# The first layer of a two-layer adaptive FFN: one written order for every engine, clamps moved to GpSimd, zero products in gaps, and pads spread over blocks

## The chip, the cores and the metric

The kernel runs on one core of one Trainium2 chip. The metric is the device time of one execution in microseconds, the median of several runs. TensorE is called PE here (its weight loads PEld), VectorE DVE, ScalarE ACT, GpSimd POOL; SyncE, which issues most transfers, is SP.

## The reference, cut to what matters

The input x has 8 batches of 512 tokens with 256 features. Two layers follow each other, each with a residual.

```python
# layer 0: a LoRA of the batch's language, then a fake-quantized FFN
y    = (x @ A[lang].T) @ Bm[lang].T + emb[lang]
xq   = round(y / sx) clipped to -128..127, times sx       # sx from max |y| over ALL of y
gate = xq @ wq(w_gate).T ; up = xq @ wq(w_up).T           # 704 columns, weights quantized by row
h    = silu(gate) * up
hq   = the same rounding, with a scale from max |h| over ALL of h
x    = x + hq @ wq(w_down).T
# layer 1: an adapter with a layer norm, then 9 experts of which each token takes 2
z = layernorm(x + relu(x @ W1 + b1) @ W2 + b2) * gamma + beta
x = x + sum over the top 2 of 9 experts of weight * (silu(z @ Wg) * (z @ Wu)) @ Wd
```

The two maxima over everything split layer 0 into parts that can't overlap: no element of y can be rounded before the last of y is known, none of h before the last of h.

## The kernel before, in words

Layer 0 keeps everything on the chip, with features on the 128 partitions. Batches go in four pairs (k = 0 to 3). In the LoRA part `lora_in(k)` makes the rank products of a pair into one two-bank PSUM tile, ACT masks them to the pair's languages (`t`), `lora_out` multiplies back, and ACT adds the embedding into `y_pairs`. DVE takes the maximum of each pair into `ymax`. Meanwhile the weights come in twice: raw by rows, from which DVE takes the row scales (`row_scales`), and transposed, which `weight_in` multiplies by the inverse scales (carried across partitions by PE in `spread`) into 16-bit integers, so that rounding happens in the conversion; a copy makes them bf16 (`wgT`, `wuT`, `wdT`). `abs_max_all` ends the part with the maximum over all partitions, and `act_scale` makes the scale `x_scale` and its inverse `x_inv`.

Rounding y is two steps: ACT writes `y * inv` as int16 into one of two buffers `v`, DVE clamps it into the bf16 tile `yq`. Gate and up are then made in chunks of 128 of the 704 columns, for one pair: five full chunks of 1024 elements a partition and a last one of 64 columns, whose two batches lie above each other (512 elements). For each chunk `gate_chunk` has eight products, `finish` takes silu on ACT, and then either DVE multiplies straight out of PSUM, or (`by_pool`, three chunks of a pair, 12 in all) ACT copies the up half out and POOL multiplies. DVE takes the maximum of each chunk into `hmax`. The four PSUM tiles rotate, as do three `g` and two `u`. The order is that in which the Python loops call these functions, and each engine works through its own share of it in order, with the scheduler switched off.

Behind the last maximum, the scale of h is made in the same way. From there a written list, `ORDER`, gives the order of all pieces: rounding of h (`qa` on ACT, `qd` on DVE), the down products (`dp`), the adapter, the routing, and the first 14 blocks of the expert stage. The routing writes each token's row, by indirect DMAs from POOL, into a list in DRAM for each of its two experts. The expert stage works on blocks of 128 rows of these lists. SP fetches for each block, in its own order: the rows (four quarters and a small `tag`), the gate and up weights (1408 KB) and the down weights (768 KB). A weight fetch is conditional: it is skipped when the buffer holds that expert already. There are three weight buffers, and rows are asked for four blocks ahead. From block 14 on, a loop calls `first_half(i)` and `second_half(i)`, in which `ask` issues the fetches.

The number of rows of an expert is known only when routing is done, so the last block of an expert has to be filled up: `write_pads` writes, for each of the nine experts, 128 rows of padding (130 KB) behind its list's end. SP reads the place from `endi` and issues the DMA. Before, all nine go out in one go ahead of block 20 (`pads_at = done + 6`):

```python
        for i in range(done, SURE):
            if i == pads_at:
                write_pads()
                asked["planned"] = NBLK
            first_half(i)
            second_half(i)
```

The list is one DRAM tensor, so that a fetch of rows waits for pads written before it, and a pad waits for rows that were fetched before it.

Of the kernel before, what the change touches and what calls it, by code (L numbers as in the profile page):

```python
# [23 lines left out]
F32 = mybir.dt.float32  # L24
# [8 lines left out]
P = 128  # L33
# [5 lines left out]

ORDER = """  # L40
# [29 lines left out]
def adaln_ffn_kernel(  # L70
# [124 lines left out]
    def rounded(dst, src, inv):  # L195

        v = in_turn("v", v_pair)
        shape = list(src.shape)[1:]
        n = shape[0] if len(shape) == 1 else shape[0] * shape[1]
        v = v[:, :n] if len(shape) == 1 else v[:, :n].rearrange("p (a b) -> p a b", b=shape[1])  # L200
        nc.scalar.activation(v, src, AF.Copy, scale=inv)
        return lambda: nc.vector.tensor_scalar(dst, v, QMAX, -QMAX - 1.0, ALU.min, ALU.max)  # L202

# [18 lines left out]

    with tc.tile_pool(name="hw", bufs=1) as hw, tc.tile_pool(
        name="wide", bufs=4, space=bass.MemoryType.PSUM
    ) as wide, tc.manual_schedule():

        def banks(name):
            return wide.tile([P, 2 * S], F32, tag="pw", name=name)


# [9 lines left out]

        taken = 0

        def piece(w, a, b):
            nonlocal taken
            raw = upper_[:, taken : taken + a * b]
            taken += a * b
            nc.sync.dma_start(raw, w)
            return raw.rearrange("p (a b) -> p a b", b=b)

        for b in range(4):  # L250
            nc.sync.dma_start(x_sb[:, b], xT[b])
        raw_g = piece(w_gate, NM, D)
        for b in range(4, B):
            nc.sync.dma_start(x_sb[:, b], xT[b])
        raw_u = piece(w_up, NM, D)
        raw_gT = piece(w_gate_T, KC, I)
        raw_uT = piece(w_up_T, KC, I)
        raw_d = piece(w_down, KC, I)
        raw_dT = piece(w_down_T, NM, D)
        assert taken <= HB // 2 * PAIR - NY  # L260
        nc.sync.dma_start(wr, Wr.rearrange("(c p) e -> p c e", p=P))
        nc.sync.dma_start(lists[E * CAP :], pad)
# [5 lines left out]

# [14 lines left out]
        hot = hw.tile([NL0, B], F32, name="hot")  # L283
        nc.vector.tensor_scalar(hot, idf[:NL0, HB:], pcol[:NL0], None, ALU.is_equal)
        emb = hw.tile([P, KC, B], F32, name="emb")
        pe = banks("pe")
        for c in range(KC):
            nc.tensor.matmul(
                pe[:, c * B : (c + 1) * B], lhsT=emb_sb[:, c * P : (c + 1) * P], rhs=hot, start=True, stop=True
            )  # L290
        nc.vector.tensor_copy(emb.rearrange("p c b -> p (c b)"), pe[:, : KC * B])
        ymax = hw.tile([P, HB], F32, name="ymax")
# [4 lines left out]
        def lora_in(k):  # L297
            pr = banks("pr")
            for c in range(KC):
                for z in range(2):  # L300
                    nc.tensor.matmul(
                        pr[z * HR : (z + 1) * HR, :S],
                        lhsT=aT[:, c],
                        rhs=x_sb[:, 2 * k + z, c],
                        start=c == 0,
                        stop=c == KC - 1,
                    )
            t = hw.tile([P, S], F32, tag="t", bufs=2, name="t")
            nc.scalar.activation(t, pr[:, :S], AF.Copy, scale=mask[:, k : k + 1])
            return t  # L310

        def lora_out(k, t):
            for c in range(KC):
                py = banks("py")
                for z in range(2):
                    zs = slice(z * HR, (z + 1) * HR)
                    nc.tensor.matmul(
                        py[:, z * S : (z + 1) * S], lhsT=bT[zs, c * P : (c + 1) * P], rhs=t[zs], start=True, stop=True
                    )
                for z in range(2):  # L320
                    b = 2 * k + z
                    nc.scalar.activation(
                        y_pairs[k][:, z, c], py[:, z * S : (z + 1) * S], AF.Identity, bias=emb[:, c, b : b + 1]
                    )


        def row_scales(name, raw, scale):

            top = hw.tile(list(scale.shape), F32, name=f"top_{name}")
            abs_max(top, raw)  # L330
            nc.vector.tensor_scalar(scale, top, 1.0 / QMAX, None, ALU.mult)
            inv = hw.tile(list(scale.shape), F32, name=f"inv_{name}")
            nc.vector.reciprocal(inv, scale)
            return inv

        def across(pi, at, col, n):

            nc.tensor.transpose(pi[:, at : at + n], col.to_broadcast([n, P]), ident[:n, :n])

        def spread(inv):  # L340
            pi = banks("pi")
            for m in range(NM):
                across(pi, m * P, inv[: rows[m], m : m + 1], rows[m])
            return pi

        def weight_in(name, raw_T, pi):
            wq = hw.tile([P, KC, I], I16, tag="wq", bufs=2, name=f"wq_{name}")
            nc.vector.tensor_tensor(wq, raw_T, pi[:, :I].unsqueeze(1).to_broadcast([P, KC, I]), ALU.mult)
            return wq.rearrange("p c i -> p (c i)")

        def abs_max_all(dst, stats, name):

            own = hw.tile([P, 1], F32, name=name)
            nc.vector.tensor_reduce(own, stats, AX.X, ALU.max)
            pi = banks("pi")
            across(pi, 0, own, P)
            nc.vector.tensor_reduce(dst, pi[:, :P], AX.X, ALU.max)

        ts = {0: lora_in(0)}
        for k in range(HB):  # L360
            if k + 1 < HB:
                ts[k + 1] = lora_in(k + 1)
            if k == 0:
                inv_g = row_scales("g", raw_g, swg)
            elif k == 3:
                inv_u = row_scales("u", raw_u, swu)
                pi_g = spread(inv_g)
                wq_g = weight_in("g", raw_gT, pi_g)
            lora_out(k, ts.pop(k))
            abs_max(ymax[:, k : k + 1], y_pairs[k].rearrange("p z c t -> p (z c t)"))  # L370
        nc.scalar.copy(wgT.rearrange("p c i -> p (c i)"), wq_g)


        ytop = hw.tile([P, 1], F32, name="ytop")
        abs_max_all(ytop, ymax, "ytop_own")
        pi_u = spread(inv_u)
        sx, rx = act_scale(ytop, sig[:, 0:1], "x")

        def round_y(b):
            return rounded(  # L380
                yq[:, b].rearrange("p c t -> p (c t)"), y_pairs[b // 2][:, b % 2].rearrange("p c t -> p (c t)"), rx
            )

        for w_scale in (swg, swu):
            nc.vector.tensor_scalar(w_scale, w_scale, sx, None, ALU.mult)
        first = round_y(0)
        second = round_y(1)
        wq_u = weight_in("u", raw_uT, pi_u)
        first()
        nc.vector.tensor_copy(wuT.rearrange("p c i -> p (c i)"), wq_u)  # L390
        second()
# [3 lines left out]
        def gate_chunk(k, m, by_pool):  # L395
            ms = slice(m * P, (m + 1) * P)
            h = h_full(k)[:, m].rearrange("p z t -> p (z t)")
            pg, pu = banks("pg"), banks("pu")
            for p, w in ((pg, wgT), (pu, wuT)):
                for c in range(KC):  # L400
                    for z in range(2):
                        nc.tensor.matmul(  # L402
                            p[:, z * S : (z + 1) * S],
                            lhsT=w[:, c, ms],
                            rhs=yq[:, 2 * k + z, c],
                            start=c == 0,
                            stop=c == KC - 1,
                        )
            finish(h, pg, pu, m, by_pool)

        def finish(h, pg, pu, m, by_pool):
            n = h.shape[1]
            g = hw.tile([P, 2 * S], F32, bufs=3, tag="g", name="g")[:, :n]
            nc.scalar.activation(g, pg[:, :n], AF.Silu, scale=swg[:, m : m + 1])  # L414
            if by_pool:
                u = hw.tile([P, 2 * S], F32, bufs=2, tag="u", name="u")
                nc.scalar.activation(u, pu[:, :n], AF.Copy, scale=swu[:, m : m + 1])  # L417
                nc.gpsimd.tensor_tensor(h, u, g, ALU.mult)  # L418
            else:
                nc.vector.scalar_tensor_tensor(h, pu[:, :n], swu[:, m : m + 1], g, ALU.mult, ALU.mult)  # L420

        def last_chunk(k):
            pg, pu = banks("pg"), banks("pu")
            for p, w in ((pg, wgT), (pu, wuT)):
# [15 lines left out]
        for k in range(HB):  # L440
# [7 lines left out]
            for second in seconds:  # L448
                second()
# [730 lines left out]
```

## Time and profile before

| what | value |
|---|---|
| median of 3 runs | 739.7 us (738.42 to 741.25) |
| profiled execution | 740.5 us, of which the profile's span is 738.4 us |
| granted PE clock, mean | 0.951 |
| PE busy | 680.9 us, 92% |
| DVE busy | 365.2 us, 49% |
| ACT busy | 203.6 us, 28% |
| POOL busy | 200.1 us, 27% |
| LoRA until `x_inv` | 0 to 33.4 us |
| gate and up until `htop_own` | 33.5 to 93.1 us |
| first down product | 98.4 us |
| one block of the expert loop on PE | 7.5 us |

The profile's lines give a start, a duration, the engine, the line of the kernel, the operation and its tiles; what stands in brackets is the idle time of the engine before it and what ended it. An SP line shows the issue of a DMA, not its transfer. PEclk is the share of full clock that PE was granted in a stretch.

### The profile page before, as it was taken

To read this page: it belongs to the slowest core of one execution; us is meant where nothing else is said; L and a number is where in the kernel's file an instruction comes from. 1 tells how busy PE (TensorE), PEld (TensorE's weight loads), DVE (VectorE), ACT (ScalarE), POOL (GpSimd) and SP (SyncE) were. 2 spreads that over 40 slices of the span, in tenths; PEclk is the share of its full clock that TensorE was granted. 3 is DMA by queue.
4 is the path that set the end of the run, shared out by engine and by line. 5 is a ranking of instruction groups with operands and counts; after the bars stand their busy time and mean duration, and the time that the engine had idled before them with its cause. 6 is when DMAs were issued, how large, how long until landed. Compare 5 with 4: busy or idle time off the path is not lost. (4 is left out here: it accounts for less than half of the span.)

```text
span 738.4 us, 14537 instructions
## 1 busy us (share of the span) xinstructions
PE 680.9 (92%) x4592; PEld 578.2 (78%) x4592; DVE 365.2 (49%) x1207; ACT 203.6 (28%) x403; POOL 200.1 (27%) x173
## 2 busy tenths in 40 slices
PE   7498669979899899899998999999999999999995
PEld 2233225536698899799997999999999999999994
DVE  3759948988957384433332333333333333333331
ACT  4577675534413031111110111111111111111110
POOL 1045500446253213452121212121212112121212
PEclk9789977879999999999999999999999999999998
DMA  9500002448757786433367623279934489135742
GB/s 347 194 1 2 0 16 64 130 166 293 257 130 235 238 261 188 76 80 42 47 166 199 162 34 44 31 209 315 296 53 106 92 275 278 30 45 151 218 98 32
DMA packets 85424, 103.44 MB, mean 140 GB/s; under 512 B 58200, under 2 KB 74720, under 8 KB 82016
## 3 DMA queue, kind: packets, MB, share of 16 engines
q1 hardware_dynamic: 72480, 85.15, 37.6%
q0 software_dynamic: 12720, 17.31, 12.2%
q8 instruction: 38, 0.62, 0.3%
q14 instruction: 42, 0.34, 0.2%
q10 hardware_dynamic: 144, 0.01, 0.0%
HBM read 176.86 MB, written 22.83 MB: 270 GB/s over the span
## 5 line engine op out<-in xcount | busy, mean ns | idle before, releaser
L974 PE MATMUL bank<-upper__104,lower 128*128 128x128 f32 x2948 | 347.3, 277 | 5.4 <-DMA lower<-in_L_ffn_W_dram 3.0
L974 PEld LDWEIGHTS bank<-upper__104,lower 128*128 128x128 f32 x2948 | 344.3, 194 | 10.0 <-issue 3.3
L1033 POOL DMA_INDIRECT out_dram<-upper__104,tag x67 | 104.5, 1560 | 373.3 <-DVE upper__104 L964 281.7
L990 DVE TENSOR_TENSOR upper__104<-bank,upper__104 128x512 f32<-128x512 f32 x67 | 46.3, 691 | 157.3 <-PE bank L974 157.3
L1023 PE MATMUL bank<-upper__104 128*128 128x256 f32 x528 | 121.4, 379 | 0.0
L1023 PEld LDWEIGHTS bank<-upper__104 128*128 128x128 f32 x528 | 97.1, 191 | 11.4
L984 ACT ACTIVATE upper__104<-bank 128x512 f32<-128x512 f32 x67 | 40.0, 597 | 233.8 <-PE bank L974 232.6
L758 POOL DMA_INDIRECT lists<-row,sloti x64 | 62.6, 979 | 97.6 <-ACT zT L672 42.1
L1000 ACT ACTIVATE upper__104<-bank 128x128 f32<-128x128 f32 x67 | 18.5, 277 | 186.1 <-PE bank L974 186.1
L1023 PE MATMUL bank<-lower,upper__104 128*128 128x256 f32 x276 | 64.0, 382 | 0.4 <-issue 0.4
L1029 DVE TENSOR_SCALAR upper__104<-bank,wt 128x256 f32<-128x256 f32 x67 | 32.4, 483 | 60.6 <-PE bank L1023 60.5
L1023 PEld LDWEIGHTS bank<-lower,upper__104 128*128 128x128 f32 x276 | 51.2, 192 | 6.9 <-issue 0.8
L1006 DVE TENSOR_TENSOR upper__104<-bank,upper__104 128x128 f32<-128x128 f32 x67 | 19.4, 290 | 71.5 <-ACT upper__104 L1001 70.3
L559 PE MATMUL bank<-yq,wdT 128*128 128x512 bf16 x80 | 25.4, 457 | 5.6 <-DVE yq L547 5.6
L414 ACT ACTIVATE g<-pg,swg 128x1024 f32<-128x1024 f32 (+1 forms) x24 | 24.8, 1048 | 9.2 <-PE pg L402 5.5
L418 POOL TENSOR_TENSOR lower<-u,g 128x1024 f32<-128x1024 f32 x6 | 14.1, 2358 | 45.8 <-ACT u L417 45.8
L402 PE MATMUL pg<-yq,wgT 128*128 128x512 bf16 x80 | 22.0, 396 | 3.7 <-DVE yq L202 2.2
L402 PE MATMUL pu<-yq,wuT 128*128 128x512 bf16 x80 | 22.1, 401 | 2.6 <-DVE lower L420 2.6
L649 ACT ACTIVATE row<-row,shift,rstd 128x256 f32<-128x256 f32 x32 | 16.8, 590 | 22.4 <-DVE shift L643 22.4
L681 PEld LDWEIGHTS bank<-wr,zT 128*128 128x128 f32 x128 | 18.3, 226 | 4.7 <-issue 3.9
L681 PE MATMUL bank<-wr,zT 128*128 128x9 f32 x128 | 18.4, 281 | 3.6 <-DVE row L623 3.4
L559 PEld LDWEIGHTS <-wdT 128*128 128x128 bf16 x80 | 8.3, 115 | 17.1 <-issue 8.0
(200 smaller groups left out, 600.9 us busy)
## 6 DMA issues: line engine op xcount, KB each, us to landing
lower<-in_L_ffn_W_dram SPq DMA_DIRECT2D x70, 1408.0 KB
upper__104<-in_L_ffn_W_dram SPq DMA_DIRECT2D x46, 768.0 KB
lower<-in_L_ffn_W_dram SPq DMA_DIRECT2D x23, 768.0 KB
lower<-lists SPq DMA_DIRECT2D x144, 32.0 KB
upper__104<-lists SPq DMA_DIRECT2D x140, 32.0 KB
x_sb<-in_x_dram SPq DMA_DIRECT2D x8, 512.0 KB
out_dram<-xtok SPq DMA_DIRECT2D x8, 512.0 KB
lists<-pad SPq DMA_DIRECT2D x10, 130.0 KB
```

The source lines that it names most:

```text
L402: nc.tensor.matmul(p[:, z * S : (z + 1) * S], lhsT=w[:, c, ms], rhs=yq[:, 2 * k + z, c], start=c == 0, stop=c == KC - 1,)
L414: nc.scalar.activation(g, pg[:, :n], AF.Silu, scale=swg[:, m : m + 1])
L559: nc.tensor.matmul(pd, lhsT=wdT[:, m, cs], rhs=hq_sb[b % 2][:, m], start=m == 0, stop=False)
L681: nc.tensor.matmul(pl[:, j * E : (j + 1) * E], lhsT=zT_sb[b % 2][:, c, j * P : (j + 1) * P], rhs=wr[:, c], start=c == 0, stop=c == KC - 1,)
L758: nc.gpsimd.indirect_dma_start(out=own_rows[(b * NJ + j) * 2 + n], out_offset=bass.IndirectOffsetOnAxis(ap=sloti_sb[b % 3][:, j, n : n + 1 ...
L974: nc.tensor.matmul(pg[:, at * P : (at + 1) * P], lhsT=gu_sb[i % NW][:, c, n * P : (n + 1) * P], rhs=xbT_sb[i % 3][:, c], start=c == 0, sto ...
L984: nc.scalar.activation(g_sb[i % 3][:, :4].rearrange("p m t -> p (m t)"), held.pop(("pg", i, "a")), AF.Silu)
L990: nc.vector.tensor_tensor(hid_sb[i % 3][:, :4].rearrange("p m t -> p (m t)"), held.pop(("pg", i, "b")), g_sb[i % 3][:, :4].rearrange("p m ...
L1006: nc.vector.tensor_tensor(hid[:, 4], pg[:, P : 2 * P], gs[:, 4], ALU.mult)
L1023: nc.tensor.matmul(po[:, :D], lhsT=hid_sb[i % 3][:, m], rhs=dn_sb[i % NW][:, m], start=m == 0, stop=m == NM - 1)
L1029: nc.vector.tensor_scalar(y_sb[i % 3], held.pop(("po", i))[:, :D], small_["wt"][i % NX], None, ALU.mult)
L1033: nc.gpsimd.indirect_dma_start(out=out, out_offset=bass.IndirectOffsetOnAxis(ap=tag_sb[i % NX][:, 0:1].bitcast(I32), axis=0), in_=y_sb[i % 3],
```

## The change

Five things change, all but the last in layer 0.

1. The LoRA, the weights and gate and up are written as small pieces with names (`li`, `t`, `lo`, `ye`, `ym` for the LoRA; `tp`, `s`, `wq`, `c` for the weights; `ox`, `tx`, `yt`, `sw` for the scale; `v`, `yr` for rounding; `gp`, `up`, `sl`, `uc`, `pm`, `st`, `mx` for the chunks; `L` for loads), and a literal list, `FRONT`, gives their order for all engines. Gate and up products of a chunk are pieces of their own, and chunks of different pairs mix. POOL multiplies 8 chunks (`pm`) instead of 12, DVE 16 (`st`). The maximum of y is taken by pair and half of the features. Row scales and weights of all three matrices now come ahead of the first product.
2. Loads are pieces too: the last pair of x is loaded behind `u`, `uT` and `gT`, and `g`, `d`, `dT` behind it.
3. Five of the eight clamps of y (`yr` with 1 at the end) run on POOL.
4. `z_n` stands for n products of a tile of zeros, written into the PSUM tile that is next in turn: 10 at the start, 6 and 2 in the LoRA, 10, 4 and 12 around the scale of y, and 12 behind the transpose that carries the maximum of h across.
5. `write_pads` becomes `write_pad(e)`, called ahead of each of the blocks 16 to 24, one pad each.

The core of the diff:

```diff
+FRONT = """
+    z_10 pe L_x0 em L_x1 z_6 li_0 L_u t_0 li_1 L_x2 lo_0_0 tp_u t_1 lo_0_1 ye_0_0 L_uT lo_1_1 ye_0_1 ym_0_0 lo_1_0
+    L_gT ye_1_1 li_2 ym_0_1 ye_1_0 ym_1_1 L_x3 s_u t_2 ym_1_0 lo_2_1 wq_u L_g lo_2_0 ye_2_1 li_3 ye_2_0 c_u L_d
+    ym_2_1 t_3 tp_g L_dT z_2 lo_3_0 lo_3_1 ye_3_0 ym_2_0 s_g ye_3_1 ym_3_0 ym_3_1 ox tp_d z_10 tx yt z_4 s_d sw v_1
+    wq_g v_0 yr_1_0 c_g yr_0_0 wq_d z_12 up_0_2 v_2 gp_0_2 v_3 c_d yr_2_1 gp_0_0 sl_0_2 gp_0_1 sl_0_0 yr_3_1 st_0_2
+    v_4 mx_0_2 up_0_0 sl_0_1 yr_4_1 up_1_0 st_0_0 v_5 up_0_1 mx_0_0 uc_1_0 gp_0_5 up_1_3 st_0_1 sl_0_5 gp_0_3
...
+    uc_3_4 up_3_3 mx_3_0 sl_3_5 gp_3_4 mx_3_2 gp_3_3 sl_3_4 mx_3_1 up_3_5 sl_3_3 pm_3_4 st_3_5 st_3_3 mx_3_3 mx_3_4
+    mx_3_5
+"""
+LAST_LOAD = "L_dT"
+ZEROS_BEHIND = 12
...
+        busy = hw.tile([P, S], BF16, name="busy")
+        nc.vector.memset(busy, 0.0)
...
+        def z(n):
+            pz = wide_sb[(turn_of.get("wide", -1) + 1) % len(wide_sb)]
+            for _ in range(n):
+                nc.tensor.matmul(pz[:, :S], lhsT=busy[:, :P], rhs=busy, start=True, stop=True)
...
+        def yr(b, by_pool):
+            (nc.gpsimd if by_pool else nc.vector).tensor_scalar(
+                yq[:, b], at.pop(("v", b)), QMAX, -QMAX - 1.0, ALU.min, ALU.max
             )
...
+        own = hw.tile([P, 1], F32, name="htop_own")
+        nc.vector.tensor_reduce(own, hmax.rearrange("p b k -> p (b k)"), AX.X, ALU.max)
+        ph = banks()
+        across(ph, own, P, 0)
+        z(ZEROS_BEHIND)
         htop = l0.tile([P, 1], F32, name="htop")
-        abs_max_all(htop, hmax.rearrange("p b k -> p (b k)"), "htop_own")
+        nc.vector.tensor_reduce(htop, ph[:, :P], AX.X, ALU.max)
...
-    def write_pads():
-        for e in range(E):
-            r = nc.sync.value_load(endi[0:1, e : e + 1], min_val=e * CAP, max_val=e * CAP + T)
-            nc.sync.dma_start(lists[ds(r, P)], pad)
+    def write_pad(e):
+        r = nc.sync.value_load(endi[0:1, e : e + 1], min_val=e * CAP, max_val=e * CAP + T)
+        nc.sync.dma_start(lists[ds(r, P)], pad)
...
-        pads_at = done + 6
+        pads_at = done + 2
         for i in range(done, SURE):
-            if i == pads_at:
-                write_pads()
+            if pads_at <= i < pads_at + E:
+                write_pad(i - pads_at)
+            if i == pads_at + E:
                 asked["planned"] = NBLK
             first_half(i)
             second_half(i)
```

## The prediction, made before the result was known

> **What bounds the kernel now.** I read the page's slices first, then the stretches that I cut at the stage borders, then the timelines of DVE, PE and SP at those borders. The chain that ended last covers only the final 18 us, so it says nothing about the stages edited here.
>
> ```profile
> PE   7498669979899899899998999999999999999995
> DVE  3759948988957384433332333333333333333331
> PEclk9789977879999999999999999999999999999998
> ```
>
> Each digit is 18.5 us. From about 300 us PE is full, and only what delays PE costs time there. In the first five slices it isn't PE that is full but DVE. The stretches (us, then busy time of PE, PEld, DVE, ACT and POOL, then PEclk) say it in numbers:
>
> ```profile
> 33.00:93.00 60.00, 45.67 (x199) 18.72 (x197) 50.23 (x56) 44.20 (x44) 28.48 (x12) 0.90 0.00 1
> 93.00:103.00 10.00, 5.07 (x13) 1.49 (x13) 4.00 (x12) 8.42 (x9) 1.01 (x2) 0.55 0.00 0
> 384.00:405.00 21.00, 18.05 (x122) 17.03 (x121) 5.76 (x20) 2.29 (x6) 3.10 (x2) 0.92 0.65 178
> ```
>
> Between 33 and 93 us (gate and up) DVE is busy 50.2 of 60. The stage ends with DVE's last maxima, and a serial chain follows until the down products start:
>
> ```profile
> 89.98 2.93 DVE L295 TENSOR_REDUCE hmax<-upper__104 128x1 f32<-128x1024 f32 x3
> 92.94 0.18 DVE L354 TENSOR_REDUCE htop_own<-hmax 128x1 f32<-128x24 f32 x1
> ...
> 98.37 2.31 PE L559 MATMUL bank<-yq,wdT 128*128 128x512 bf16 x5 [4.67 <-DVE yq L547]
> ```
>
> PE had finished its gate products at 87.1; the granted clock is half from 91.9 to 102.1. The third place is the expert loop at 384 to 405, where the pads go out:
>
> ```profile
> 352.73 0.08 SPq L943 DMA_DIRECT2D lower<-in_L_ffn_W_dram  x1
> 354.12 2.52 SPq L933 DMA_DIRECT2D upper__104<-lists  x4
> ...
> 370.23 0.35 SPq L943 DMA_DIRECT2D lower<-in_L_ffn_W_dram  x1
> 372.06 9.51 SPq L895 DMA_DIRECT2D lists<-pad  x9
> 384.29 2.27 SPq L933 DMA_DIRECT2D lower<-lists  x4
> 386.83 0.35 SPq L936 DMA_DIRECT2D tag<-lists  x1
> 388.84 0.35 SPq L943 DMA_DIRECT2D lower<-in_L_ffn_W_dram  x1
> ```
>
> ```profile
> 389.51 2.76 PE L1023 MATMUL bank<-lower,upper__104 128*128 128x256 f32 x12
> 395.22 6.78 PE L974 MATMUL bank<-upper__104,lower 128*128 128x128 f32 x44 [2.95 <-DMA lower<-in_L_ffn_W_dram]
> 401.83 2.75 PE L1023 MATMUL bank<-upper__104 128*128 128x256 f32 x12
> ```
>
> An SP row of 0.08 us at L943 is a skipped weight load (same expert as before), one of 0.35 a real one. The burst holds SP for 12 us, the real load of block 23 goes out at 388.84, and PE stands 2.95 us for it. The clock then halves: the 44 products take 6.78 us where other blocks take 5.08. Cost of the burst: 2.95 + 1.70, with rounding 4.8 us (block 24 starts at 404.4, where 7.5 us a block gives 399.6).
>
> **LoRA.** The list loads `u`, `uT` and `gT` ahead of the last pair of x and `g` behind it: 1408 KB more in front, at the 1.27 us per 512 KB between the landings of x, so that pair lands at 20.4 instead of 17.0. Then in order: `li_3` behind the pair-2 products, `t_3` about 24.4, `lo_3` 25.1, four activations of 0.6 to 28.7, last `ym` 1.2 to 29.9. `tp_d` (1.61 + 0.17 + 0.19) now stands between `ox` and `yt` on DVE, to 32.1, and `yt` ends at 32.8. Before: 33.4. Gain 0.6; up to 2.0 if `tp_d` fits under the zeros. The split `ym` and the extra zeros hide under x's landings.
>
> **Gate and up.** From the scale, ACT sets the first product: two `v` (2 x 1.05), the `g` cast 1.36 (its `wq_g` needs 1.62 on DVE, inside that), two more `v`, one silu 1.1, so DVE's first `st` starts 6.6 after x_inv, at 39.4. PE's zeros end before `yr_0` is there. From then DVE holds 12 full `st` (four products leave POOL for DVE, four more casts leave ACT) at 1.20 from start to start, 4 half ones at 0.66, 20 full maxima at 1.17, 4 half at 0.60, one clamp 0.34: 14.4 + 2.6 + 23.4 + 2.4 + 0.3 = 43.2. With 0.8 idle it ends at 83.4 instead of 92.9: 9.5 less, 0.6 of it from LoRA. What goes from DVE: `top_d`, `wq_d` and `wdT` (3.9, now in front, in the 1.7 us gap before the first `st` or on `yt`'s path), five clamps, and two clamps and a 128x2 scale that stood behind POOL's products:
>
> ```profile
> 46.18 1.99 DVE L202 TENSOR_SCALAR yq<-v 128x1024 bf16<-128x1024 int16 x2 [0.23 <-ACT v L201]
> ...
> 57.70 1.77 DVE L331 TENSOR_SCALAR swd<-top_d 128x2 f32<-128x2 f32 x1
> ```
>
> (alone 0.84 and 0.17). ACT has 24 silu, 8 casts, 8 `v`, one weight cast, about 41 us, and PE 38 us at full clock: both under DVE. The queued work that could turn this around is POOL's: a clamp of 128x1024 is on no row. Below: nothing, since POOL has idle time; above: the product of two such inputs, 2.36. I take something between, since a clamp reads one input, and walking the list row by row with 2.36 moves the end by 0.2 only; at 4 us it would move by 5, because gate products of pairs 1 to 3 wait for it.
> The Trainium skill, "GPSIMD Engine Reference" (section 3.1), says that one-input work of two operations runs at about 1.03 cycles an element at 1.2 GHz, an estimate of 0.9 us for a clamp; no row here shows it, and by it the sum would lose the 0.2. The same page's advice to leave elementwise work on VectorE speaks against the move.
>
> **Behind the stage.** htop's chain to the first down product stays at 5.4 us. Twelve zeros (128x512 products at 0.216 full, 0.43 half clock, as in the gate rows: 2.6 or 5.1 us) lie in PE's 4.67 us gap. If they hold the clock, the 3.7 us of half clock after 98.37 shrink by 1.9; if they don't, nothing, and at half clock they may push the first product by 0.5. I take 1.0. Front in all: 9.5 + 1.0 = 10.5 (7 to 11.5).
>
> **The pads.** Now one pad precedes each block's rows, blocks 16 to 24. In the built program each pad waits for the previous rows' landing and the next rows wait for that pad's; behind that wait on SP stand the rows, the tag, gate-up and down weights. Without a pad SP needs 5.46 us a block (347.25 to 352.73) against PE's 7.50, and works off a lag: its gate-up issue leads PE by 7.3 us at block 18 (347.25 against 354.58), 9.4 at 19, 14.4 at 22 (370.23 against 384.60). With a pad, rows start 0.95 (register load, issue) + landing + 0.1 after the down issue instead of 0.8. The last pads land 2.3 to 2.9 after issue (in the rows above, the ninth pad's issue ends at 381.57 and rows go at 384.29). With 2.3 each pad costs 2.55, SP's round 8.0 us, so the lead shrinks instead of growing. Real loads land 6.24 after issue (block 23's). Walking it:
> Gate-up 22 issues at 370.23 + 4 x 2.55 = 380.4, lands 386.7, due 384.6: 2.1 late, 1.7 for the clock. Pad 4 queues behind that load (in before the first pad landed 1.3 after it), so gate-up 23 issues at 391.8, lands 398.0, due 395.9: 2.1 + 1.7. Pad 5 waits behind load 23 and down 22; block 24 is skipped and in time; 25 is 0.4 late. Gate-up 26 issues at 423.1, lands 429.3, due 422.6: 6.7 + 1.7. Sum 16.4; less the 4.8 that vanish: +11.6. With 2.0 a pad and 6.2 a load it is +8, with 2.9 and the 7.5 to 8.5 that loads 22 and 26 took, +16. If pads were waited for by nobody, the sum would be -4.8.
> The Trainium skill, "DMA: Bandwidth & Descriptors" (section "Two DMAs through the same engine are not ordered"), says that a read after a write must wait for the write's completion even on one queue: nine separate round trips, where the burst pays one. Its fit, 2.0 us + bytes/436e3, makes an estimate of 2.3 for a pad, and the sum would be +11.6 by it.
>
> **Sum.** Against the profiled execution's 740.5: -10.5 + 11.6 = +1.1. That execution is 0.8 above the median 739.7, so I predict 740.8. Half a percent is 3.7 us, about what a measurement of this kernel can tell from no change.
>
> **Rivals.** *Faster: the pads stay hidden.* SP must be further ahead when the pads start, or their landing must overlap its register loads. For it: before shows SP gaining 2 us a block. Against: the wait is in the program, the lag at block 18 comes from the order in front, which is unchanged. Then -10.5 - 4.8: 724; if only load 26 is late (6.7 + 1.7 - 4.8), 733.
> *Slower: SP's round trips cascade.* Place: SP, blocks 20 to 26, where pads stand behind 1408 KB loads. Price: +16 with landings of 2.9 and loads of 7.5 to 8.5; 740 - 10.5 + 16 gives 745 to 746. It decides from a landing of about 2.6 (pads over 14.2). For it: loads 22 and 26. Against: those loads shared the queue with the burst or rows. A slow POOL clamp (4 us) adds 5 on the same side.
> *The zeros don't hold the clock:* +1, inside the forecast.
>
> **Numbers.** Forecast (736 to 743.4) 0.50; faster 0.24; slower 0.26. Own range 735 to 745. To hold 8 in 10 it reaches half into the faster case (729) and through the cascade (748). Chances by sign: faster 0.24, same 0.50, slower 0.26.
>
> **What would show it.** Right: `htop_own` near 83.4, DVE idle under 2 us from 39 to 83, first down product near 89 with 0.22 us products; SP rows at about 8 us a block under pads; PE gaps for L_ffn_W at blocks 22, 23 and 26. Wrong: POOL clamps over 2.4 us with PE waiting on them, a DVE end after 86, rows that don't wait for the pad, or no PE gap between blocks 18 and 28.

## The result and the profile after

The changed kernel takes 738.02 us in the median (733.5 to 742.3, 20 runs) against 740.25 us (736.48 to 744.92, 20 runs): a ratio of 0.9966, 95% interval 0.9945 to 0.9986. That is a small gain where a small loss (740.8) was predicted. Here and below a ratio and its interval leave out the executions more than 1.5% above a kernel's fastest, which the medians include, so the two can differ by a few tenths of a per cent. The profiled execution took 737.45 us with a span of 735.6, against 740.5 and 738.4. The 2.8 us are a difference of two large terms of opposite sign. Block 14, the first of the block loop, starts on PE at 310.5 instead of 324.6 (-14.1), and the 52 blocks from there to the last one take 406.4 us instead of 395.0 (+11.4).

The page's slices after the change:

```profile
PE   9989798699899998999979699999999999999995
DVE  4999779889682844333323133333333333333331
PEclk9999898689999999999999899999999999999999
```

In the first two slices PE is busy 9 tenths where it had 7 and 4: the zeros fill it. The new low spots are the 21st and the 23rd slice (368 to 386 and 405 to 423 us): these are the spread pads.

The stretches of the changed kernel, cut at its own borders (us, then busy time of PE, PEld, DVE, ACT and POOL, then PEclk), are gate and up, the chain to the first down products, and the pads:

```profile
30.50:81.70 51.20, 42.97 (x205) 17.05 (x202) 48.61 (x50) 41.33 (x41) 24.73 (x13) 0.99 0.02 6
81.70:91.80 10.10, 9.94 (x31) 3.41 (x31) 5.53 (x15) 8.65 (x9) 1.26 (x2) 0.73 0.01 2
360.00:430.00 70.00, 57.88 (x403) 54.33 (x402) 18.87 (x65) 8.56 (x23) 10.86 (x7) 0.93 0.53 136
```

DVE still bounds gate and up, now 48.6 of 51.2 us. In the chain the mean clock is 0.73 where it was 0.55. Under the pads PE loses 12 of 70 us.

The timelines at the same steps, each row with its start and duration. First the LoRA: on PE the first rank products and the last `lo`, on DVE `tp_d` and the scale:

```profile
7.60 4.14 PE L346 MATMUL wide<-x_sb,small_sb 128*64 128x512 f32 x16
...
23.06 1.99 PE L364 MATMUL wide<-t,small_sb 64*128 64x512 f32 x8 [0.30 <-ACT t L357]
...
28.03 1.61 DVE L308 TENSOR_REDUCE top_d<-upper__104 128x2 f32<-128x1408 f32 x1
...
30.51 0.17 DVE L139 RECIPROCAL x_inv<-x_scale 128x1 f32<-128x1 f32 x1
```

The first 16 products take 4.14 us; in the trace of before the same 16 took 6.64. `x_inv` starts at 30.51 instead of 33.24. Behind gate and up:

```profile
81.57 0.18 DVE L530 TENSOR_REDUCE htop_own<-hmax 128x1 f32<-128x24 f32 x1
...
82.07 5.28 PE L327 MATMUL wide<-busy 128*128 128x512 bf16 x12
87.41 1.24 PE L624 MATMUL bank<-yq,wdT 128*128 128x512 bf16 x5
```

`htop_own` is 11.4 earlier (92.94 before). The twelve zeros run at half speed themselves (0.44 each), and the down products behind them at full speed: 1.24 for five instead of 2.31. Then SP's issues under the pads:

```profile
359.16 0.38 SPq L959 DMA_DIRECT2D lists<-pad  x1
361.16 1.91 SPq L997 DMA_DIRECT2D upper__104<-lists  x4
...
365.23 0.35 SPq L1007 DMA_DIRECT2D lower<-in_L_ffn_W_dram  x1
...
367.04 0.36 SPq L959 DMA_DIRECT2D lists<-pad  x1
373.38 1.89 SPq L997 DMA_DIRECT2D lower<-lists  x4
```

A pad's rows go 2.0 us after its issue here when no real weight load is under way (2.0 to 3.4 over the pads of that kind), and 6.3 us after it when the gate-up load of 365.23 (1408 KB) went out just ahead. SP waits for a pad nine times, 24.1 us in all and 5.2 at most. The four waits on PE that follow from this, and their line in the sum of waits:

```profile
373.33 6.78 PE L1038 MATMUL bank<-upper__104,lower 128*128 128x128 f32 x44 [2.65 <-DMA lower<-in_L_ffn_W_dram]
...
384.06 5.15 PE L1038 MATMUL bank<-upper__104,lower 128*128 128x128 f32 x44 [1.36 <-DMA lower<-in_L_ffn_W_dram]
...
400.20 5.15 PE L1038 MATMUL bank<-upper__104,lower 128*128 128x128 f32 x44 [0.89 <-DMA lower<-in_L_ffn_W_dram]
...
415.16 6.63 PE L1038 MATMUL bank<-upper__104,lower 128*128 128x128 f32 x44 [7.22 <-DMA lower<-in_L_ffn_W_dram]
```

```profile
PE bank L1038 <- DMA lower<-in_L_ffn_W_dram: 12.1, 4, 7.2
```

The waits are at blocks 22, 23, 25 and 26, and behind the first and the last of them the products run in part at half clock (6.78 and 6.63 for 5.07; mean granted clock 0.75 and 0.76).

### The profile page after: what moved, and what is told of

It reads as the page before. It is cut to its first block, busy times and chain, and to the rows that moved or that the text cites. A ratio compares the mean times of both kernels' runs of the same rounds, so it can differ in the third digit from the quotient of the medians.

```text
span 735.6 us, 14657 instructions
## 1 busy us (share of the span) xinstructions
PE 685.3 (93%) x4648; PEld 577.4 (78%) x4648; DVE 367.3 (50%) x1211; ACT 198.8 (27%) x399; POOL 197.1 (27%) x174
## 3 DMA queue, kind: packets, MB, share of 16 engines
q0 software_dynamic: 12720, 17.31, 12.6%
## 5 line engine op out<-in xcount | busy, mean ns | idle before, releaser
L1038 PE MATMUL bank<-upper__104,lower 128*128 128x128 f32 x2948 | 347.1, 277 | 14.6 <-DMA lower<-in_L_ffn_W_dram 12.1
L1087 PEld LDWEIGHTS bank<-upper__104 128*128 128x128 f32 x528 | 97.6, 192 | 11.6
L498 ACT ACTIVATE g<-wide,swg 128x1024 f32<-128x1024 f32 (+1 forms) x24 | 24.1, 1040 | 3.1 <-PE wide L474 2.8
L624 PE MATMUL bank<-yq,wdT 128*128 128x512 bf16 x80 | 22.4, 412 | 1.0 <-DVE yq L612 0.9
L1028 DVE STREAM_TRANSPOSE upper__104<-lower 128x128 f32<-128x128 f32 x72 | 17.9, 287 | 10.1 <-DMA lower<-lists 9.0
L474 PE MATMUL wide<-yq,wuT 128*128 128x512 bf16 x80 | 19.6, 379 | 2.7 <-DVE lower L511 2.3
L1028 DVE STREAM_TRANSPOSE upper__104<-upper__104 128x128 f32<-128x128 f32 x64 | 15.9, 287 | 12.3 <-DMA upper__104<-lists 12.2
L1072 DVE TENSOR_TENSOR upper__104<-bank,upper__104 64x128 f32<-64x128 f32 x67 | 19.7, 294 | 2.0
L746 PEld LDWEIGHTS bank<-wr,zT 128*128 128x128 f32 x128 | 16.7, 209 | 4.1 <-issue 3.1
L746 PE MATMUL bank<-wr,zT 128*128 128x9 f32 x128 | 16.8, 268 | 3.1 <-DVE row L688 2.7
```

What stands on the lines that cost most here:

```text
L498: nc.scalar.activation(g, pg, AF.Silu, scale=swg[:, m : m + 1])
L624: nc.tensor.matmul(pd, lhsT=wdT[:, m, cs], rhs=hq_sb[b % 2][:, m], start=m == 0, stop=False)
L746: nc.tensor.matmul(pl[:, j * E : (j + 1) * E], lhsT=zT_sb[b % 2][:, c, j * P : (j + 1) * P], rhs=wr[:, c], start=c == 0, stop=c == KC - 1,)
L1028: nc.vector.transpose(xbT_sb[i % 3][:, c], xb_sb[i % NX][:, :, c * 32 : (c + 1) * 32])
L1038: nc.tensor.matmul(pg[:, at * P : (at + 1) * P], lhsT=gu_sb[i % NW][:, c, n * P : (n + 1) * P], rhs=xbT_sb[i % 3][:, c], start=c == 0, sto ...
L1072: nc.vector.tensor_tensor(hid[up, 5], pg[up, 2 * P : 3 * P], gs[up, 5], ALU.mult)
```

## The experiments

Three series were run, and each ratio is against the kernel before in the same series. The level differs between them: in the second series the kernel before took 741.38 us, as in the result; in the first and third it took 756.95 and 757.65 us with a wider spread, so that intervals are wide there and small terms are read from the traces. The table shows where the profiled executions pass five points (start of `x_inv`, of `htop_own`, of the first and the 25th down product and of block 14, us).

| kernel | x_inv | htop_own | first down | 25th down | block 14 |
|---|---|---|---|---|---|
| before | 33.24 | 92.94 | 98.4 | 113.6 | 324.6 |
| after | 30.51 | 81.57 | 87.4 | 100.8 | 310.5 |
| e1, pads in one burst | 31.49 | 82.56 | 87.9 | 101.8 | 331.6 |
| e2, before with spread pads | 34.03 | 94.19 | 99.6 | 115.3 | 342.1 |
| e3, late pads | 31.41 | 82.47 | 88.4 | 102.4 | 328.8 |
| e4, no zeros | 33.12 | 85.30 | 90.7 | 106.5 | 332.6 |
| e6, late pads again | 30.48 | 81.53 | 87.2 | 101.1 | 311.5 |
| e7, late pads, no zeros | 31.32 | 83.23 | 88.6 | 104.0 | 314.2 |
| e8, late pads, zeros of the LoRA alone | 30.66 | 83.09 | 88.5 | 104.2 | 312.1 |
| e9, late pads, `tp_d` later | 30.19 | 84.59 | 90.2 | 104.1 | 313.8 |
| e10, before with late pads | 33.64 | 93.91 | 99.3 | 115.0 | 340.4 |
| e11, late pads, clamps on DVE | 31.21 | 82.88 | 88.5 | 102.4 | 334.9 |
| e12, the changed kernel again | 31.16 | 82.22 | 87.6 | 101.5 | 328.6 |
| e13, before with zeros | 33.20 | 94.68 | 100.2 | 113.7 | 345.7 |

### First series: the front and the pads apart

**The changed kernel with the pads in one burst again.**

```diff
-        pads_at = done + 2
+        pads_at = done + 6
...
-            if pads_at <= i < pads_at + E:
-                write_pad(i - pads_at)
-            if i == pads_at + E:
+            if i == pads_at:
+                for e in range(E):
+                    write_pad(e)
```

> The changed kernel with its pads put back as they were: all nine in one go ahead of block 20. Theory A (the front gains 14 us by the start of block 14, the spread pads lose 10.7 of it): the stalls of PE for weights fall from 12.1 to about 3 us, and the time is 740.2 - 14 = 726, ratio to before 0.981. Rival B (the pads cost nothing either way, the front gains only the 2.5 us that the whole change shows): 738, ratio 0.997.

Measured: 745.82 us, ratio 0.9835 (0.9783 to 0.9888). The front alone gains some 12 us in this series (8 to 16), and spreading the pads takes that away again.

**The kernel before with the pads spread, and nothing else.**

```diff
-        pads_at = done + 6
+        pads_at = done + 2
...
-            if i == pads_at:
-                write_pads()
+            if pads_at <= i < pads_at + E:
+                write_pad(i - pads_at)
+            if i == pads_at + E:
```

> The kernel before with nothing changed but the pads, one ahead of each of the blocks 16 to 24. Theory A: PE waits at blocks 22, 23, 25 and 26 as in the changed kernel, some 12 us in all and 3 for the clock behind the long ones, where before lost 4.8: 10.7 slower, 751, ratio 1.0145. Rival B: 740, ratio 1.000. A gain (735, the 4.8 gone) would say that the waits of the changed kernel come from its front.

Measured: 768.26 us, ratio 1.0142 (1.0098 to 1.0185), the size that was expected. From block 22 to 27 four blocks take 10.0, 8.2, 14.2 and 10.3 us instead of 7.5: spreading is a loss with either front. The waits differ from the expectation: PE waits for weights twice, at blocks 23 and 26 (2.31 and 6.48 us), not four times. Over 7.5 a block it is 12.7 us from block 15 on, where the burst costs 2.3 in this series (kernel above). Block 14 takes 11.7 us besides, with no pad near it.

**The changed kernel with the pads one a block, but from block 26 on.**

```diff
-        pads_at = done + 2
+        pads_at = done + 12
```

> The changed kernel with pads_at = done + 12: one pad a block, ahead of blocks 26 to 34, where SP's issue of gate and up leads PE by up to 17.4 us and no real weight load comes until block 37. Theory A (a pad costs SP 2.5 to 3 us wherever it stands, and only the small lead and the real loads of blocks 22, 23 and 26 turn that into waits of PE): no stall at 20 to 30, 740.2 - 14 - 4.8 = 721, ratio 0.975. Rival D (SP's round of 8 to 9 us against PE's 7.5 stalls PE anywhere): stalls move to blocks 30 to 38, and the time stays near 738, ratio 0.997.

Measured: 745.59 us, ratio 0.986 (0.9815 to 0.9906). The time lies between the two expectations and just outside both. The trace has no weight wait: every block from 15 on takes 7.5 us. It gains nothing over the burst here: in this series the burst's one stall cost only 2.3 us (4.8 in the trace of before), and in this execution block 14 takes 10.6 us, because PE stops three times in it (0.45, 0.95 and 1.03 us) for nothing that the profile names. Such a block 14 stands in four traces of the first and third series (this one, 10.6; before with spread pads, 11.7; without zeros, 12.3; before with late pads, 10.1) and in no other. Its cause isn't shown.

**The changed kernel without zeros.**

```diff
-            for _ in range(n):
-                nc.tensor.matmul(pz[:, :S], lhsT=busy[:, :P], rhs=busy, start=True, stop=True)
+            del pz
```

> The changed kernel without its products of zeros (z makes none). Theory C (the zeros hold the clock, and my sum had the LoRA at half clock): LoRA's first products run at 0.43 instead of 0.25 us, x_inv comes 1 to 2 us later (32 instead of 30.7), the first down products run at half clock for 3 to 4 us; 3 to 5 us more in all, ratio to before 1.001 to 1.004. Rival (the zeros only fill gaps): x_inv within 0.5 us, ratio 0.997; if they stood in the way, 0.99.

Measured: 756.24 us, ratio 0.9986 (0.9953 to 1.0019). The time by itself tells nothing, since pad stalls and this series' spread lie over it. The trace does: `x_inv` stands at 33.12 where the two kernels above with zeros have 31.49 and 31.41. Half of that, 0.83, is a wait for a load of x. This row raised the question of the second series.

### Second series: what the zeros are worth

All four keep the pads late, so that no pad stall lies over the front.

**The base again** (the same edit as in the kernel with pads from block 26 on).

> The changed kernel with the pads one a block from block 26 on, run again as the base of this series, so that what follows is not blurred by pad stalls. Theory Z (the zeros' warm clock is what the front term missed): ratio about 0.986 as in its first run, x_inv near 31, no PE wait for L_ffn_W above 0.5 us from block 15 on. Rival R (the front is worth what was forecast, 10.5 us, and the rest is drift of chip and run): ratio 0.98 to 0.99 all the same; this run alone does not part them.

Measured: 721.58 us (719.71 to 723.55), ratio 0.9732 (0.9711 to 0.9754). Both expectations had more, 0.98 to 0.99; the same kernel stood at 0.986 in the first series, and of that difference only the 3.1 us of block 14 are placed. The block loop, PE's timeline at two blocks where the changed kernel waits:

```profile
371.57 5.08 PE L1038 MATMUL bank<-upper__104,lower 128*128 128x128 f32 x44
...
379.07 5.07 PE L1038 MATMUL bank<-upper__104,lower 128*128 128x128 f32 x44
```

There is no idle time in brackets and 7.50 us from start to start; the 52 blocks from 14 on take 390.2 us. The pads still take their round trips (a pad issued at 403.19, its rows at 405.40), but by then SP is far enough ahead.

**Without zeros.** The edit is the one of the kernel without zeros above, on this base.

> The same without any product of zeros. Theory Z: x_inv 1.6 to 2.1 us later, the first 24 down products 1.8 us longer, the chain from htop_own to the first of them 0.5 shorter, together 3 to 4 us, a ratio 0.004 to 0.005 above that of the base (0.990 to 0.992). Rival R: the zeros are worth under 1 us at the end (ratio within 0.001 of the base), because what the warm clock gains early is given back when the throttle takes its half-clock stretches later.

Measured: 726.24 us (724.79 to 726.72), ratio 0.9799 (0.9784 to 0.9814): the zeros are worth 4.7 us. In the profiled pair it is 2.6 (spans of 720.3 and 722.9). PE's timeline without zeros:

```profile
5.93 6.77 PE L345 MATMUL wide<-x_sb,small_sb 128*64 128x512 f32 x16
...
88.60 2.31 PE L623 MATMUL bank<-yq,wdT 128*128 128x512 bf16 x5 [4.67 <-DVE yq L611]
```

The rank products are back at 0.42 us each and the first down products at half clock. Row by row of the table, leaving out the zeros costs 0.84 until `x_inv`, 0.86 until `htop_own`, gains 0.3 in the chain (the zeros no longer stand in front of the first product) and costs 1.5 in the first 24 down products: 2.8, of which 2.6 are still there at block 14. The two profiled executions differ by 2.6 in time too (722.2 and 724.79 us), so the other 2.1 of the medians are not in this pair.

**With the zeros of the LoRA alone.**

```diff
-ox tp_d z_10 tx yt z_4 s_d
+ox tp_d z_0 tx yt z_0 s_d
...
-wq_d z_12 up_0_2
+wq_d z_0 up_0_2
...
-ZEROS_BEHIND = 12
+ZEROS_BEHIND = 0
```

> The same with the zeros of the LoRA alone (10, 6 and 2); those around the scale of y and behind the transpose of h's maximum are left out. Theory Z: x_inv as in the base (within 0.3 us), the first down products at half clock again, so 0.5 to 1.5 us at the end: ratio 0.001 to 0.002 above the base. If the later zeros are what counts, it lies with the kernel without zeros, 0.004 above.

Measured: 723.64 us, ratio 0.9765 (0.975 to 0.978), 2.1 us above the base and 2.6 below none. `x_inv` stays early (30.66), but `x_inv` to `htop_own` takes 52.4 instead of 51.1 and the first 24 down products 15.7 instead of 13.9. So those around the scale of y carry the start of gate and up, and those behind h's maximum the down products, together a little more than I expected. What the zeros of the LoRA are worth at the end is not placed: against none at all, `x_inv` comes 0.66 earlier, but `x_inv` to `htop_own` takes 52.4 against 51.9, and the 25th down product starts at 104.1 against 104.0. The 2.6 between the times arise behind it (block 14 at 312.1 against 314.2), where no zeros stand.

**`tp_d` behind the scale.**

```diff
-ox tp_d z_10 tx yt z_4 s_d sw v_1
+ox z_10 tx yt z_4 sw v_1
-wq_g v_0 yr_1_0 c_g yr_0_0 wq_d z_12 up_0_2 v_2 gp_0_2 v_3 c_d yr_2_1 gp_0_0 sl_0_2 gp_0_1 sl_0_0 yr_3_1 st_0_2
-v_4 mx_0_2 up_0_0 sl_0_1
+wq_g v_0 yr_1_0 c_g yr_0_0 tp_d z_12 up_0_2 v_2 gp_0_2 s_d v_3 wq_d c_d yr_2_1 gp_0_0 sl_0_2 sl_0_0 yr_3_1 st_0_2
+v_4 mx_0_2 up_0_0 gp_0_1 sl_0_1
```

> The base with the row scales of w_down (tp_d, 1.61 + 0.17 + 0.17 us on DVE) taken from between ox and yt to behind yr_0_0, its transposes (s_d) behind gp_0_2, and gp_0_1 behind up_0_0. Theory: tp_d holds yt by 1.5 us, so x_inv 1.4 us earlier; DVE's gap ahead of the first st (1.66 us) takes tp_d, so htop_own 1.0 to 1.5 earlier, ratio 0.002 below the base. Rival: x_inv earlier, but DVE pays it back (2.0 us more in front of the stage that it bounds): htop_own within 0.4 us, ratio equal.

Measured: 724.27 us, ratio 0.9773 (0.9756 to 0.979): worse than the base by 2.7. From `ytop_own` to `x_inv` it is 1.4 shorter, as expected (in this execution the loads came about 1.1 us later, which hides it in the table). But from `x_inv` to `htop_own` it is 3.3 longer. DVE's timeline:

```profile
33.01 1.61 DVE L308 TENSOR_REDUCE top_d<-upper__104 128x2 f32<-128x1408 f32 x1
...
44.55 1.28 DVE L511 SCALAR_TENSOR_TENSOR lower<-wide,swu,g 128x1024 f32<-128x1024 f32 x1 [1.74 <-PE wide L474]
```

and ACT's:

```profile
41.74 1.11 ACT L498 ACTIVATE g<-wide,swg 128x1024 f32<-128x1024 f32 x1 [2.72 <-PE wide L474]
```

`tp_d` does go into the gap ahead of the first `st`, but with what depends on it fills more than the gap: the first `st` starts 7.6 us behind `x_inv` instead of 6.8. Then, with `gp_0_1` behind `up_0_0`, ACT is without a gate chunk for 2.72 us and DVE without work for 1.74. The other 0.8 is not placed. Both expectations missed. The likely reason is the PSUM tile that the moved transposes take: ahead of `up_0_0` PE waits 2.77 us for the `st` that frees one (1.59 in the base). No run tests it apart.

### Third series: the burst, the clamps, and zeros alone

**The kernel before with late pads.** The edit is that of the kernel before with spread pads, with `done + 12`.

> The kernel before with one change: the nine pads go out one a block ahead of blocks 26 to 34 instead of in one burst ahead of block 20. Theory P (pads cost what the profile of before shows, 2.95 of wait and 1.70 of half clock, and nothing where SP is far enough ahead): ratio about 0.993 (4.8 of 740), no PE wait for L_ffn_W above 0.5 us from block 15 on. Rival: the stall's time comes back elsewhere, ratio 1.000.

Measured: 753.87 us, ratio 0.9945 (0.9911 to 0.998), or 4.2 us less (1.5 to 6.7). No block from 15 on takes more than 7.5 us (block 14 takes 10.1). The burst is worth about what the profile of before shows, within a wide interval.

**All clamps on DVE**, with late pads:

```diff
-c_d yr_2_1 gp_0_0 sl_0_2 gp_0_1 sl_0_0 yr_3_1 st_0_2
+c_d yr_2_0 gp_0_0 sl_0_2 gp_0_1 sl_0_0 yr_3_0 st_0_2
...
```

(likewise for batches 4, 6 and 7).

> The changed kernel with late pads (as in the earlier series) and all eight clamps of y on DVE, in the places that the list gives them. Theory: five clamps of 0.42 us come to DVE, which bounds the stage, so htop_own comes 1.7 to 2.1 us later and the ratio is 0.002 to 0.003 above the one of late pads alone (0.973 on the chip of that series). Rival: POOL's clamps (1.04 to 1.2 us each) hold the products of their batch 0.7 us longer than DVE's would, so that half or more comes back: within 0.001.

Measured: 744.58 us, ratio 0.9842 (0.9786 to 0.9898), too wide for a term of this size. By the traces `x_inv` to `htop_own` takes 51.67 instead of 51.06 in the changed kernel beside it: 0.6, not 1.7 to 2.1. DVE's timeline shows part of the reason:

```profile
36.30 0.42 DVE L453 TENSOR_SCALAR yq<-v 128x1024 bf16<-128x1024 int16 x1
37.04 0.43 DVE L453 TENSOR_SCALAR yq<-v 128x1024 bf16<-128x1024 int16 x1 [0.32 <-ACT v L449]
38.04 1.28 DVE L511 SCALAR_TENSOR_TENSOR lower<-wide,swu,g 128x1024 f32<-128x1024 f32 x1 [0.57 <-ACT g L498]
```

Two of the five clamps lie in the gap ahead of the first `st`, which ACT sets; the other three cost 0.33 each from start to start, 1.0 of which 0.4 comes back at a place not found. On POOL a clamp takes 1.04 to 1.2 us, in the timeline of the changed kernel:

```profile
35.35 2.34 POOL L453 TENSOR_SCALAR yq<-v 128x1024 bf16<-128x1024 int16 x2 [31.74 <-ACT v L449]
39.42 1.04 POOL L453 TENSOR_SCALAR yq<-v 128x1024 bf16<-128x1024 int16 x1 [1.73 <-ACT v L449]
```

**The changed kernel again.**

> The changed kernel itself, on the chip and in the rounds of this series. If pads one a block from block 16 cost what the walk says (16.4 us in all) and what the traces of the changed kernel show (15.5), it lies about 0.021 above the changed kernel with late pads and near 0.995 of the kernel before. Rival (the pads' price was overread and the changed kernel gains 2% on a quiet chip): below 0.985.

Measured: 757.14 us, ratio 0.998 (0.9937 to 1.0024). It is 0.0138 above the kernel with late pads and clamps on DVE of the same series (the one without that change of clamps was not run in it), less than the 0.021 expected, with intervals of some 0.005 on each. Its trace has 14.3 us over 7.5 a block (blocks 22 to 27), so the mechanism is the same, and its size here is a little smaller: PE waits twice for weights (3.89 and 6.18 us) instead of four times. The rival, a gain of over 1.5%, is out.

**The kernel before with zeros alone.**

```diff
+            for _ in range(n):
+                nc.tensor.matmul(tile_[:, :S], lhsT=busy[:, :P], rhs=busy, start=True, stop=True)
...
         pe = banks("pe")
+        zeros(pe, 10)
...
             pr = banks("pr")
+            zeros(pr, 6 if k == 0 else 0)
...
             pi = banks("pi")
+            zeros(pi, ahead)
             across(pi, 0, own, P)
+            zeros(banks("pz"), behind)
```

> The kernel before with products of zeros and nothing else: 10 ahead of the embedding's products, 6 ahead of the first pair's, 32 ahead of and 12 behind the transpose of y's maximum, 12 behind that of h's. Its order, clamps and pads stay. Theory Z: the zeros are worth in the old order what they are worth in the new one, 3 to 5 us: ratio 0.993 to 0.996, the first 16 rank products at 0.25 us or less each instead of 0.42, the first 24 down products 1.5 us shorter. Rival: in the old order the LoRA is held by loads and by DVE, so only the gain behind h's scale is left, 1 to 2 us (0.998).

Measured: 761.21 us, ratio 1.0033 (0.9991 to 1.0074): no gain. The rank products are as fast as in the changed kernel (first row, PE), and yet `x_inv` comes at the old time (33.20):

```profile
7.85 4.27 PE L309 MATMUL pr<-x_sb,small_sb 128*64 128x512 f32 x16
...
32.42 2.75 PE L273 MATMUL pz<-busy 128*128 128x512 bf16 x12
```

In the old order DVE ends the LoRA (6.93 busy of the 7 us from 24 to 31 in the trace of before), so a faster PE ahead of it moves nothing. The first 24 down products take 13.5 instead of 15.2, as expected. That this last gain is not in the time has one reason in the trace. The twelve zeros behind the transpose of y's maximum (second row above) stand on PE in front of the transposes that DVE needs for the weights of up. DVE's timeline of before, then of this run:

```profile
34.03 1.62 DVE L348 TENSOR_TENSOR wq_u<-upper__104,pi 128x1408 int16<-128x1408 f32 x1 [0.36 <-PE pi L338]
```

```profile
35.96 1.62 DVE L356 TENSOR_TENSOR wq_u<-upper__104,pi 128x1408 int16<-128x1408 f32 x1 [2.33 <-PE pi L346]
```

From `x_inv` to `htop_own` it is 61.5 us instead of 59.7 (60.3 in e10), so these zeros give back most of what those behind h's maximum gain, and the 25th down product stands at 113.7 (113.6 and 115.0). Zeros that are out of the way there were not run. Block 14 starts 5 us later than in e10, most of it behind the down products; where that comes from isn't settled.

## Why the prediction was wrong

**Where it went wrong: the term for the front.** The sum had -10.5 for everything ahead of the blocks; the profile has -14.1 (-13.0 in the trace of the base of the second series, whose front is the same), outside the bounds of 7 to 11.5. The step that failed is the LoRA's, with the zeros in it put at nothing: 2.1 of the 3.6 us that the term lacked. By its steps:

- *LoRA, "Gain 0.6".* Measured 2.7. The walk put `lo_3` at 25.1 and the last `ym` at 29.9; they stand at 23.06 and at about 27.9. The step said that "the extra zeros hide under x's landings", that is, that they are worth nothing. In the second series they are worth 0.8 of the 2.8 us between before and the base (30.48 against 31.32), in the first 1.6 to 1.7, the wait for x among it. The other 1.3 that the step lacked are the walk itself, which had the last pair's products too late: without any zeros `lo_3` starts at 23.88. The place of `tp_d`, between `ox` and `yt`, was as walked (28.03, and `ytop` behind it at 29.96).
- *Gate and up, "9.5 less" at the stage's end, 83.4.* The end came at 81.57. From `x_inv` it is 51.06 us against the 50.6 of the walk (first `st` 6.8 behind `x_inv`, predicted 6.6), so this part of the sum held within 0.5. Without zeros it is 51.9, so some 0.8 of it leans on them, which the step did not count.
- *Behind the stage, "I take 1.0".* The choice between "they hold the clock" (1.9) and "they don't" (0) went to the middle. They hold it (granted clock 1.00 from 87.4 to 92): 1.8 in the first 24 down products, less 0.4 because the zeros, at half speed, end at 87.35 and push the first product (5.84 instead of 5.43), as the step said they may. Between the first down product and block 14 there are 3.1 us in all, 1.8 of it in these products; the other 1.3 spread over the written order. The kernels of the second series gain between 0.6 and 2.6 over the whole of that stretch, so I give the 1.3 no cause.

So of the 3.6 us, 2.1 lie in the LoRA, 0.3 in the chain and the first down products, and 1.4 behind these without a cause; gate and up had 0.3 too much. The zeros were mis-sized: 1.0 for all three groups, measured 2.6 to 2.8 in the traces and 4.7 in the times (some 3 to 7 by the intervals of the two ratios). Without zeros the front is worth -10.4 in the trace (314.2 against 324.6 at block 14), where the sum without its 1.0 had 9.5. The times show this in one series; in the first the traces up to the 25th down product point the same way (106.5 without, 101.8 and 102.4 with), and its times are too wide to tell. What the written order, the order of the loads and the four products moved from POOL to DVE are worth each was not tested apart.

**What held: the pads.** The walk gave 16.4 of stalls, less 4.8 for the burst that vanishes, +11.6. Measured against the 390.2 us of the blocks without a stall: 16.2, less before's 4.8, +11.4. The places were right (blocks 22, 23, 25, 26), and so was the largest one (7.22 of wait, 6.7 walked). The burst's price was tested by itself (-4.2), the spread by itself (+1.4% on the old front), and the whole by leaving both out: 721.58, 19.8 under the kernel before of its series, of which the traces place 13.0 in the front and 4.8 in the burst. Inside the sum two sizes were off and cancel, which is luck: the waits are 12.1 instead of 11.3, and the 1.7 of half clock stands behind two of them, not three.

**The rule on the GpSimd clamp.** The Trainium skill, "GPSIMD Engine Reference" (section 3.1), led to an estimate of 0.9 us a clamp against the row's upper bound of 2.36. The trace has 1.04 to 1.2, so the page's figure is nearer, and a little low. Its general advice is to keep elementwise work on VectorE, and a clamp is slower on POOL (0.42 on DVE); the move is still worth 0.6 us by the traces, in a stage that DVE bounds.

**The rule on the pads.** "DMA: Bandwidth & Descriptors" (section "Two DMAs through the same engine are not ordered") says that a read of what a transfer wrote must wait for that transfer's completion. The page's fit, which it gives for transfers issued from GpSimd (section "Anatomy of one DMA — SWDGE (gpsimd) path"), gave an estimate of 2.3 us for a pad, which SP issues. In the trace SP's rows wait for all nine pads; no run leaves the wait out. The times are 2.0 to 3.4 with no real load ahead of the pad, and 5.5 to 6.3 behind a 1408 KB load. The first kind makes the load of block 22 late; the second delays those behind it, and the walk had it as "queues behind that load".

**The rivals.** "The pads stay hidden" is refuted by the four waits. "Round trips cascade" had the place right and too high a price. "The zeros don't hold the clock" is refuted by the down products at 1.24 for five.

**Two readings.** Of the first five slices DVE is full only in the fourth and fifth (9 tenths); in the LoRA it has 3 and 7. SP's block from 347.25 to 352.73 takes 5.48 us, not 5.46. Neither moves the sum.

## What to carry to other kernels

A gain in a serial front and a loss in a saturated loop add up at their full sizes, so cost them apart and test them apart: here a change of 0.3% was -14 and +11, and moving the nine pads ten blocks later took the stalls away (0.973 in one series, the lowest ratio of all kernels run, and 0.986 in another). Work that only keeps an engine's clock up has a price by place: ask at each place whether that engine ends the stage, and whether another engine waits for what comes behind. Zeros gained 3 to 5 us in the new order; in the old one faster rank products did not move `x_inv`, and twelve zeros in front of a transpose cost 1 to 2 us. A write that later reads must wait for is cheap or dear by what is queued in front of it and by how far the issuing queue is ahead, not by its own 2 us.

## What the runs showed of the hardware

- The profile's granted clock read 1.00 in the first 8 us while PE's products ran at half speed: zeros of 128x512 took 0.41 at the start and 0.245 from 6.2 us on, and without zeros (second series) the rank products ran at 0.42 until 12.6. The slow start isn't in PEclk; only the durations show it.
- Zeros run at half speed too while the clock is halved (5.28 us for 12, granted clock 0.51), and the products behind them are fast (1.24 for five, granted clock 1.00). Products of zeros were enough to bring the clock back.
- The level of a series differs by place. In the two that took 757 us for the kernel before, the stretch from the first down product to block 14 took 240 to 246 us instead of 223 to 226, with or without any part of this change, while the stages up to the first down product and the blocks took nearly the same. The record has the second and the third series on one chip (7), so the chip alone doesn't explain it. The cause isn't shown.
